# A transformer block in one kernel: PSUM banks of one tag taken in turn by three, the row of maxima moved to ScalarE, sixteen small sums moved to VectorE, two idle products fewer

## Chip, cores and metric

The kernel runs on one core of one Trainium2 chip. The metric is the device time of one launch in microseconds, the median of the runs. Smaller is better.

## What is computed

A block of a diffusion transformer on 16 batches of 256 tokens with 256 features, 16 heads of 16 features each, everything in float32:

```
shift_a, scale_a, gate_a, shift_m, scale_m, gate_m = split(silu(c) @ W_mod + b_mod, 6)
q, k, v = split(modulate(ln(x), shift_a, scale_a) @ W_qkv + b_qkv, 3)
x = x + gate_a * (softmax(q k^T / 4) v @ W_proj + b_proj)            # self-attention, 256 x 256 per head
q = ln(x) @ W_qc + b_qc;  k, v = split(ln(context) @ W_kvc + b_kvc, 2)
x = x + softmax(q k^T / 4) v @ W_cproj + b_cproj                     # cross-attention, 256 context rows
x = x + gate_m * (gelu(modulate(ln(x), shift_m, scale_m) @ W_mlp1 + b_mlp1) @ W_mlp2 + b_mlp2)
```

`ln(t) = (t - mean) * rsqrt(var + 1e-6)`, and `modulate(t, shift, s) = t * (1 + s) + shift`.

## The kernel before

**Units and beats.** The attention work is cut into 32 units: a self-attention unit (kind `s`) and a cross-attention unit (kind `c`) for each batch, in the order s0 to s4, then s5, c0, s6, c1 and so on, and c11 to c15 at the end. The main loop runs over the units `n`, and in each over eight beats `k` (`beat(n, k)`, line 1076). Almost every instruction is pinned to the program order of its engine, so the order written in `beat` is the order in which each engine works.

In beat `k` of unit `n`, `visit` (line 1054) puts on TensorE:
- the scores of unit n+1 for the maxima, four products into the tile `sp` (shown as `s` in the profile), which VectorE reduces to `mx`;
- the transposed scores of unit n for a pair of heads, four products into `st`, of which ScalarE takes the exponential into `pt` (`exp`, called through `exps()`).

Beside these, a beat holds work for other units. In beats 0, 2, 4 and 6, `av_part` multiplies the exponentials with v (tile `o`, 16 products on 32 columns each), and some beats have transposes of normalised inputs (`psT_...`). The projections run as "lanes" (line 444): each product is done in halves of 64 rows, and two projections share the array, one in the upper half of the rows and one in the lower half. `lanes(x, y)` starts x and finishes y, and `run` issues its twelve steps. The order is Q of unit n+2 from beat 1 on, the output projection P of unit n-2 from beat 3, K of unit n+3 from beat 5, and V of unit n+3 from beat 6 or 7.

**The row of maxima.** The softmax subtracts a maximum that is put as a row of its own into q: `m_turn` transposes `mx` on TensorE, `m_row` negates it, and a DMA from SP's queue writes it into q. For the second half of a unit this is in beat 0, for the first half of the next unit in beat 4. When the unit three ahead is a cross-attention unit (`lx` is set), beat 4 writes the transpose into `sp[:, 0]`, ahead of the four transposes of `lx.T[1].turn()`, and `m_row` works on VectorE between the two halves of `q2.Q.low`. Otherwise it has a tile of its own (`psm_...`), and `m_row` works on ScalarE.

**PSUM.** `st` and `sp` take two banks each. The other four banks are shared by two tags, `gen` (`LONG`) and `tr` (`SHORT`), with two buffers each. The projections and the first MLP product take `LONG`; the transposes, `o` and `psm` take `SHORT`. A tile waits until the buffer that it is given has been read.

**Low parts.** Projections are done in three products of rounded high and low parts. `Q.high` rounds on ScalarE (`h_q`, `h_qc`), and `Q.low` subtracts on VectorE (`l_q`, `l_qc`); with these two a projection's bank has been read. The same holds for K.

**Layer norms.** `layernorm` (line 312) takes statistics on VectorE (`st_`, `mv_`), adds epsilon and takes the power -1/2 on GpSimd (`rs_`, in `pow`), and applies both on GpSimd (`xn_`). The names `c0` to `c15` and `q0` to `q15` are those of the context and of the cross-attention's queries.

**Beginning and end.** The beginning is a list of words in `PRE`, issued in order; the word `b12` is twelve products of zeros on TensorE (`busy`, tile `wz`), of two weight loads each, ahead of the transpose of the bias rows (`brow`) and that of the activated condition (`turn`). After the units, the MLP runs over chunks of hidden features, with `mlp_first` (tile `ph`), two gelu passes on ScalarE, a subtraction on GpSimd, and `mlp_second` into `sp` and `st` in turn.

All operations are recorded through one helper, so that the profile gives them line 51; they are told apart by the names of their tiles.

Of the kernel before, what the change touches and what calls it, by code (L numbers as in the profile page):

```python
# [21 lines left out]
def pixart_block(  # L22
# [29 lines left out]
                return tc.keep_in_program_order(i) if self.on else i  # L52
            return issue

    E_ = {'M': ((-46, -37, -26, -24, -20), (-26, -17, -10, -8, 1), (-3, 1, 4, 7, 9), (8, 11, 13, 15)), 'LN': {'s': 'pool', 'c': 'pool', 'q': 'pool'}, 'ON': (1, 1, 1), 'H': (7, 11, 14, 15), 'AP': 23, 'DV': (1, 2), 'E': (-14, -6, -2, 2), 'HP': (1, 0, 2), 'W1P': [(-9, 3), (-8, 3), (-7, 3), (-6, 3), (-4, 5), (-4, 7), (-3, 1), (-3, 5)], 'W2P': [(-4, 3), (-4, 7), (-3, 2), (-3, 4), (-3, 6), (-3, 7), (-2, 2), (-2, 4), (-2, 6), (-1, 0)], 'PRE': 'z0qp z0kp load ld2 ld3 rest one0 silu b12 brow L0a turn L0b b1 L0d scale hik lok T0t z1kp b2 shift T0h T0l ldm hiq loq hiv b1 bk K0a K0m L1a L1b lov L2a L2b z1qa bq K0h K0x K0ya L1e K0l K0s Q0a Q0m Q0h Q0x0 Q0y0a T1t Q0l Q0s0 Q0r T1h V0a V0b T1l bv L2c L3a L3b L3p L3c K1a K1b', 'SL': {(-1, 0): 'Q1a Q1b K1x K1y K1l K1s', (-1, 1): 'T2t T2h T2p V1a Q1x Q1y Q1l Q1s', (-1, 2): 'V1b cpm2', (-1, 3): 'rest z2ka', (-1, 4): 'M0 rest one1 ld4', (-1, 5): 'K2a vone', (-1, 6): 'K2m z2qa', (-1, 7): 'rest c1 one2', (0, 0): 'cpm0 b3 rest', (0, 1): 'rest', (0, 4): 'rest', (1, 0): 'rest', (1, 2): 'rest', (1, 4): 'rest'}}
# [7 lines left out]
    psum = ctx.enter_context(tc.tile_pool(name="psum", bufs=2, space=bass.MemoryType.PSUM))  # L63

    LONG, SHORT = "gen", "tr"
    ps_turn = [0]

    def ps_gen(name, tag=None):


        if tag is None and ps_turn[0] is not None:
            ps_turn[0] ^= 1
            tag = (SHORT, LONG)[ps_turn[0]]
        tag = tag or SHORT
        return psum.tile([P, 512], F32, tag=tag, name=name, bufs=2)


    wz = const.tile([P, P], F32, name="wz")
# [230 lines left out]
    class Box:  # L309
        pass  # L310

    def layernorm(src, name):

        o = Box()
# [12 lines left out]
                o.pow()  # L327

        def pow():
            POOL.tensor_scalar(o.rs, o.mv[:, :, 1], EPS, None, ALU.add)  # L330
            POOL.tensor_tensor(o.rs, o.rs, mhalf, ALU.pow)

        def apply(eng=E_['LN'].get(name[0])):
# [141 lines left out]
    def to_stack(W, src, bias, dst, which, name):  # L475
# [24 lines left out]
        def low(between=None):  # L500
            if name == "k0":
                gap(work, 64, "gap_l")
            o.lo = work.tile([P, KC, N], F32R, tag="qkl", name=f"l_{name}", bufs=3)
            if name == "k0":
                gap(work, 192, "gap_mx")
            for f in range(KC):
                if f and between:
                    between()
# [32 lines left out]
    def to_v(W, src, vt, name):  # L541
        o = Box()
        o.W, o.src, o.tok, o.name = W, src, True, f"v_{name}"

        def first():
            o.ps = ps_gen(f"psv_{name}", SHORT)
            mm3_tok(o.ps[:, 0:H], src.xT, 0, W)

        def second():
            mm3_tok(o.ps[:, H:], src.xT, 1, W)  # L550
            keep()

# [174 lines left out]
        PE.transpose(pst[:16, :P], u.mx[:, hf].rearrange("p r a t -> p (r a t)"), ident)  # L727
        return pst

    def m_row(u, hf, pst, dve=False):  # L730

        m = work.tile([16, P], F32R, tag="m", name=f"m_{u.n}_{hf}", bufs=1)
        if dve:
            DVE.tensor_scalar(m, pst[:16, :P], -1.0, None, ALU.mult)
        else:
            ACT.mul(m, pst[:16, :P], -1.0)
        SP.dma_start(u.q[63:P:64, 4 * hf:4 * hf + 4, :].bitcast(F32), m.bitcast(F32))

    def t_part(u, pair, par):
# [23 lines left out]
    def in_turn(*pieces):  # L763

        for _ in range(2):
            for f in pieces:
                next(f)
# [308 lines left out]
    def beat(n, k):  # L1076
# [20 lines left out]
        if k == 6:  # L1097
            if q2 and not n:
                q2.V.keep()
            if p2 and not alone:  # L1100
                p2.end()
        visit(n, k)
        if k == 0:
            exps()
            if prev:
# [66 lines left out]
        elif k == 4:  # L1172
# [16 lines left out]
            if q3 and q3.kind == "c":  # L1189
                q3.T[0].rest_pool()  # L1190
# [4 lines left out]
                ls.ready = True  # L1195
        elif k == 5:
            exps()
            run(lanes(q3 and q3.K, (None if alone else p2) if n else q2.V))
            if cur:
                o_out(cur, 0)  # L1200
            if lc:
# [38 lines left out]
                p2.add()  # L1240
                p2.store()

    ps_turn[0] = None
    for n in range(-1, nu):
        ACT.on = E_['ON'][0] or n >= nu - 1
        for k in range(8):
# [98 lines left out]
```

## Time and profile before

| | |
|---|---|
| median of 3 runs | 726.04 us (725.52 to 727.03) |
| the profiled execution | 726.2 us |
| its span, first to last instruction | 724.4 us |
| granted TensorE clock, mean | 0.998 |
| TensorE products busy | 712.4 us, 98% of the span |
| TensorE weight loads busy | 592.1 us, 82% |
| VectorE busy | 563.6 us, 78% |
| ScalarE busy | 553.1 us, 76% |
| GpSimd busy | 542.8 us, 75% |

A row of the timeline gives the start in us from the span's start, the duration, the engine (PE is TensorE, PEld its weight loads, DVE VectorE, ACT ScalarE, POOL GpSimd, SP the queue of SyncE), the line, the operation, the tiles as out<-in, the shapes, the count, and in brackets the idle time before it with what ended it. A product's weight load starts just before the product, so PEld rows show when TensorE takes up a piece of work. "issue" is idle time for which the profile shows no wait.

### The profile page before, as it was taken

How to read it: one execution, taken by the hardware profiler on the slowest of the kernel's cores; microseconds unless marked ns; L12 is line 12 of the kernel's file. 1: busy time of each engine (PE TensorE's matmuls, PEld its weight loads, DVE VectorE, ACT ScalarE, POOL GpSimd, SP SyncE). 2: the span in 40 equal slices, each digit the busy share in tenths (PEclk: the TensorE clock that was granted, in tenths of full speed). 3: DMA queues.
4: the chain of work that ended last, by engine and by line, in shares of the span. 5: the costliest groups of instructions: out<-in, count | busy, mean ns of one | idle time of the engine just before them, and what ended most of it. 6: DMA issues, size and time to landing. Idle time of an engine off the chain costs nothing.

```text
span 724.4 us, 22550 instructions
## 1 busy us (share of the span) xinstructions
PE 712.4 (98%) x9007; PEld 592.1 (82%) x9007; DVE 563.6 (78%) x892; ACT 553.1 (76%) x955; POOL 542.8 (75%) x533
## 2 busy tenths in 40 slices
PE   9999999999999999999999999999999999999996
PEld 8777777777777777777777777777679999999996
DVE  5878888888888888888888888888665777777743
ACT  5577888888888888888888888888767677666661
POOL 8465688887867867787786898998766989666561
PEclk9999999999999999999999999999999999999999
DMA  8465455554545555453555656455332223322122
GB/s 261 154 211 175 151 167 176 173 163 165 186 137 179 171 188 171 165 186 135 193 166 184 200 167 201 150 192 190 92 92 87 84 62 85 69 66 88 55 49 73
DMA packets 81531, 106.14 MB, mean 147 GB/s; under 512 B 16594, under 2 KB 44532, under 8 KB 81428
## 3 DMA queue, kind: packets, MB, share of 16 engines
q1 hardware_dynamic: 80420, 104.12, 44.4%
q8 instruction: 71, 1.16, 0.7%
q10 hardware_dynamic: 1008, 0.59, 0.3%
q14 instruction: 32, 0.26, 0.1%
HBM read 35.89 MB, written 8.98 MB: 62 GB/s over the span
## 4 chain that ended last, share of the span: by engine, by line
PE 93%; DVE 4%; ACT 1%; DMA 1%; issue 1%; SPq 0%; ACTq 0%
PE s L51 19%; PE o L51 15%; PE st L51 14%; PE ph L51 12%; PE ps_k L51 4%; PE ps_qc L51 3%; PE ps_q L51 3%; PE ps_v_c L51 3%; PE ps_kc L51 3%; PE ps_P_s L51 3%; DVE mx L51 3%; PE ps_v_s L51 3%; PE ps_P_c L51 2%; PE psT_c L51 2%; PE psT_s L51 2%; PE psT_m L51 1%
## 5 line engine op out<-in xcount | busy, mean ns | idle before, releaser
L51 DVE TENSOR_REDUCE mx<-s 128x4 f32<-128x1024 f32 x252 | 307.9, 1222 | 83.0 <-PE s L51 78.8
L51 ACT ACTIVATE pt<-st 128x1024 f32<-128x1024 f32 x256 | 264.2, 1032 | 58.1 <-PE st L51 56.8
L51 PE MATMUL o<-pt,v 128*32 128x256 f32 x2048 | 137.0, 385 | 0.0
L51 PE MATMUL s<-big 63*128 63x256 f32 x1008 | 117.2, 306 | 2.2 <-DVE mx L51 0.8
L51 PE MATMUL st<-big 64*128 64x256 f32 (+1 forms) x1040 | 107.0, 280 | 0.7 <-ACT pt L51 0.7
L51 PE MATMUL ph<-xTh_m,wself 128*128 128x256 f32 x512 | 99.5, 280 | 0.0
L51 POOL TENSOR_TENSOR hl<-hf,hh 128x512 fp32r<-128x512 f32 x60 | 81.0, 1368 | 19.7 <-ACT hh L51 19.7
L51 PEld LDWEIGHTS s<-big 63*128 63x128 f32 x1008 | 77.4, 185 | 21.8 <-issue 8.5
L51 PEld LDWEIGHTS o<-pt,v 128*32 128x32 f32 x2048 | 53.4, 109 | 39.2
L51 PEld LDWEIGHTS st<-big 64*128 64x128 f32 (+1 forms) x1040 | 81.5, 186 | 3.6 <-ACT pt L51 2.1
L51 PEld LDWEIGHTS ph<-xTh_m,wself 128*128 128x128 f32 x512 | 82.0, 188 | 1.2 <-issue 0.4
L51 PE MATMUL ph<-xTl_m,wself 128*128 128x256 f32 x256 | 70.9, 277 | 0.0
L51 ACT ACTIVATE hh<-ph,bT 128x256 fp32r<-128x256 f32 x112 | 47.4, 479 | 19.0 <-PE st L51 7.4
L51 ACT ACTIVATE hf<-ph,bT 128x256 f32<-128x256 f32 x112 | 47.2, 475 | 19.3 <-PE ph L51 19.2
L51 PEld LDWEIGHTS ph<-xTl_m,wself 128*128 128x128 f32 x256 | 48.2, 188 | 0.0
L51 PE MATMUL s<-big,hh 128*128 128x256 f32 x256 | 45.2, 277 | 0.0
L51 DVE TENSOR_SCALAR xn_m<-x,mv_m,rs_m 128x256 f32<-128x256 f32 x28 | 33.5, 1236 | 14.8 <-POOL rs_m L51 14.8
L51 POOL TENSOR_SCALAR xn_c<-c,mv_c,rs_c 128x256 f32<-128x256 f32 x32 | 39.0, 1229 | 1.7
L51 PE MATMUL st<-big,hh 128*128 128x256 f32 x224 | 39.5, 276 | 0.0
L51 POOL TENSOR_SCALAR xn_q<-x,mv_q,rs_q 128x256 f32<-128x256 f32 x31 | 37.8, 1229 | 1.7
L51 ACT COPY oT<-o 128x512 f32<-128x512 f32 x64 | 37.6, 587 | 1.4 <-PE o L51 1.4
L51 PEld LDWEIGHTS s<-big,hh 128*128 128x128 f32 x256 | 38.6, 188 | 0.0
(229 smaller groups left out, 2121.1 us busy)
## 6 DMA issues: line engine op xcount, KB each, us to landing
big<-h_kc SPq DMA_DIRECT2D x32, 256.0 KB
big<-h_qc SPq DMA_DIRECT2D x32, 256.0 KB
big<-h_k SPq DMA_DIRECT2D x31, 256.0 KB
big<-h_q SPq DMA_DIRECT2D x30, 256.0 KB
big<-l_k SPq DMA_DIRECT2D x16, 256.0 KB
g<-gd SPq DMA_DIRECT2D x16, 256.0 KB
U_s<-oT SPq DMA_DIRECT2D x32, 128.0 KB
c<-in_ctx_dram SPq DMA_DIRECT2D x16, 256.0 KB
```

Of the source, the lines that this page charges most:

```text
L51: i = f(*a, **k)
```

## The change

- The tag `SHORT` has three buffers, and `LONG` one. Q, K and the first MLP product take `SHORT`; the projections to token rows (V and P) and most of the MLP's transposes take `LONG`. Transposes, `o` and `psm` stay with `SHORT`.
- In beat 4 with `lx`, the transpose of the maxima goes into `st[:, 0]`, behind the four transposes, and `m_row` works on ScalarE. In beat 5 with `lx`, two of the twelve lane steps are issued between the products of `s` and those of `st`.
- For the norms `c8` to `c15` and `q8` to `q15` epsilon is added on VectorE, as (var + eps) max var; the power stays on GpSimd.
- `b12` in the beginning is `b10`.

```diff
-    E_ = {... 'PRE': 'z0qp z0kp load ld2 ld3 rest one0 silu b12 brow L0a turn ...
+    E_ = {... 'PRE': 'z0qp z0kp load ld2 ld3 rest one0 silu b10 brow L0a turn ...
...
-    ps_turn = [0]
-    def ps_gen(name, tag=None):
-        if tag is None and ps_turn[0] is not None:
-            ps_turn[0] ^= 1
-            tag = (SHORT, LONG)[ps_turn[0]]
-        tag = tag or SHORT
-        return psum.tile([P, 512], F32, tag=tag, name=name, bufs=2)
+    def ps_gen(name, tag=SHORT):
+        return psum.tile([P, 512], F32, tag=tag, name=name, bufs=1 if tag == LONG else 3)
...
+    eased = [f"{c}{b}" for c in "cq" for b in range(8, B)]
...
         def pow():
-            POOL.tensor_scalar(o.rs, o.mv[:, :, 1], EPS, None, ALU.add)
+            if name in eased:
+                DVE.scalar_tensor_tensor(o.rs, o.mv[:, :, 1], EPS, o.mv[:, :, 1], ALU.add, ALU.max)
+            else:
+                POOL.tensor_scalar(o.rs, o.mv[:, :, 1], EPS, None, ALU.add)
             POOL.tensor_tensor(o.rs, o.rs, mhalf, ALU.pow)
...
-            x.ps, x.fresh = ps_gen(f"ps_{x.name}", LONG), True
+            x.ps, x.fresh = ps_gen(f"ps_{x.name}", LONG if x.tok else SHORT), True
...
-            o.ps = ps_gen(f"ps_{name}", LONG)         # to_stack: Q, K
+            o.ps = ps_gen(f"ps_{name}", SHORT)
...
-            o.ps = ps_gen(f"psv_{name}", SHORT)       # to_v
+            o.ps = ps_gen(f"psv_{name}", LONG)
...
-        pst = ps_gen(f"psT_m{b}", LONG if b < 2 else SHORT)
+        pst = ps_gen(f"psT_m{b}", SHORT if b == 2 else LONG)
...
-        ph = ps_gen(f"ph_{b}_{c}", LONG).rearrange("p (j n) -> p j n", j=2)
+        ph = ps_gen(f"ph_{b}_{c}", SHORT).rearrange("p (j n) -> p j n", j=2)
...
-    def visit(n, k, home=sp):
+    def visit(n, k, home=sp, between=None):
...
         in_turn(*s)
+        if between:
+            between()
         in_turn(*t)
...
-        visit(n, k)
+        kp = None
+        if k == 5 and lx and n:
+            kp = lanes(q3.K, None if alone else p2)
+        visit(n, k, between=kp and (lambda: run(kp, 2)))
...
-            if nxt:
-                pst = m_turn(nxt, 0, sp[:, 0] if lx else None)
             if lx:
                 lx.T[1].turn()
-            if nxt and not lx:
-                m_row(nxt, 0, pst)
+            if nxt:
+                m_part(nxt, 0, st[:, 0] if lx else None)
             if q2:
-                q2.Q.low((lambda: m_row(nxt, 0, pst, True)) if lx else None)
+                q2.Q.low()
...
-            run(lanes(q3 and q3.K, (None if alone else p2) if n else q2.V))
+            run(kp or lanes(q3 and q3.K, (None if alone else p2) if n else q2.V))
```

More of the change, by code (lines that the diff above doesn't have):

```diff
@@ L53, in __getattr__ @@
             return issue
-    E_ = {'M': ((-46, -37, -26, -24, -20), (-26, -17, -10, -8, 1), (-3, 1, 4, 7, 9), (8, 11, 13, 15)), 'LN': {'s': 'pool', 'c': 'pool', 'q': 'pool'}, 'ON': (1, 1, 1), 'H': (7, 11, 14, 15), 'AP': 23, 'DV': (1, 2), 'E': (-14, -6, -2, 2), 'HP': (1, 0, 2), 'W1P': [(-9, 3), (-8, 3), (-7, 3), (-6, 3), (-4, 5), (-4, 7), (-3, 1), (-3, 5)], 'W2P': [(-4, 3), (-4, 7), (-3, 2), (-3, 4), (-3, 6), (-3, 7), (-2, 2), (-2, 4), (-2, 6), (-1, 0)], 'PRE': 'z0qp z0kp load ld2 ld3 rest one0 silu b12 brow L0a turn L0b b1 L0d scale hik lok T0t z1kp b2 shift T0h T0l ldm hiq loq hiv b1 bk K0a K0m L1a L1b lov L2a L2b z1qa bq K0h K0x K0ya L1e K0l K0s Q0a Q0m Q0h Q0x0 Q0y0a T1t Q0l Q0s0 Q0r T1h V0a V0b T1l bv L2c L3a L3b L3p L3c K1a K1b', 'SL': {(-1, 0): 'Q1a Q1b K1x K1y K1l K1s', (-1, 1): 'T2t T2h T2p V1a Q1x Q1y Q1l Q1s', (-1, 2): 'V1b cpm2', (-1, 3): 'rest z2ka', (-1, 4): 'M0 rest one1 ld4', (-1, 5): 'K2a vone', (-1, 6): 'K2m z2qa', (-1, 7): 'rest c1 one2', (0, 0): 'cpm0 b3 rest', (0, 1): 'rest', (0, 4): 'rest', (1, 0): 'rest', (1, 2): 'rest', (1, 4): 'rest'}}
+    E_ = {'M': ((-46, -37, -26, -24, -20), (-26, -17, -10, -8, 1), (-3, 1, 4, 7, 9), (8, 11, 13, 15)), 'LN': {'s': 'pool', 'c': 'pool', 'q': 'pool'}, 'ON': (1, 1, 1), 'H': (7, 11, 14, 15), 'AP': 23, 'DV': (1, 2), 'E': (-14, -6, -2, 2), 'HP': (1, 0, 2), 'W1P': [(-9, 3), (-8, 3), (-7, 3), (-6, 3), (-4, 5), (-4, 7), (-3, 1), (-3, 5)], 'W2P': [(-4, 3), (-4, 7), (-3, 2), (-3, 4), (-3, 6), (-3, 7), (-2, 2), (-2, 4), (-2, 6), (-1, 0)], 'PRE': 'z0qp z0kp load ld2 ld3 rest one0 silu b10 brow L0a turn L0b b1 L0d scale hik lok T0t z1kp b2 shift T0h T0l ldm hiq loq hiv b1 bk K0a K0m L1a L1b lov L2a L2b z1qa bq K0h K0x K0ya L1e K0l K0s Q0a Q0m Q0h Q0x0 Q0y0a T1t Q0l Q0s0 Q0r T1h V0a V0b T1l bv L2c L3a L3b L3p L3c K1a K1b', 'SL': {(-1, 0): 'Q1a Q1b K1x K1y K1l K1s', (-1, 1): 'T2t T2h T2p V1a Q1x Q1y Q1l Q1s', (-1, 2): 'V1b cpm2', (-1, 3): 'rest z2ka', (-1, 4): 'M0 rest one1 ld4', (-1, 5): 'K2a vone', (-1, 6): 'K2m z2qa', (-1, 7): 'rest c1 one2', (0, 0): 'cpm0 b3 rest', (0, 1): 'rest', (0, 4): 'rest', (1, 0): 'rest', (1, 2): 'rest', (1, 4): 'rest'}}
     PE = InOrder(nc.tensor, True)
@@ L498, in high, with low @@
                 ACT.activation(o.hi[:, f], o.ps[:, f * N:(f + 1) * N], AF.Identity, bias=bias[f])
-        def low(between=None):
+        def low():
             if name == "k0":
@@ L506, in low @@
             for f in range(KC):
-                if f and between:
-                    between()
                 DVE.scalar_tensor_tensor(o.lo[:, f], o.ps[:, f * N:(f + 1) * N], bias[f], o.hi[:, f],
@@ L728, in m_turn, with m_row @@
         return pst
-    def m_row(u, hf, pst, dve=False):
+    def m_row(u, hf, pst):
         m = work.tile([16, P], F32R, tag="m", name=f"m_{u.n}_{hf}", bufs=1)
[L733 to L736, printed above, removed]
+        ACT.mul(m, pst[:16, :P], -1.0)
         SP.dma_start(u.q[63:P:64, 4 * hf:4 * hf + 4, :].bitcast(F32), m.bitcast(F32))
@@ L1241, in beat @@
                 p2.store()
-    ps_turn[0] = None
     for n in range(-1, nu):
```

## The prediction

> **What bounds the kernel now.** I read the page first, then the list of waits and the answers by tile, then the timeline of single beats, one engine at a time.
>
> ```profile
> span 724.4 us, 22550 instructions
> PE 93%; DVE 4%; ACT 1%; DMA 1%; issue 1%; SPq 0%; ACTq 0%
> ```
>
> TensorE carries 93% of the chain that ended last. What a change is worth is therefore how long TensorE stands still at the places it touches. The profiled execution took 726.2, which is 1.8 more than its span and 0.2 above the median of 726.04; I add the differences to the median.
>
> In every beat TensorE has s (scores for the maxima), st (scores for the exponentials), projections, and in even beats the products with v. VectorE must reduce s and ScalarE must take the exponential of st before the next beat may write there, so three engines run in step. Two kinds of beat 4 to 5 matter. In one, the unit three ahead is a self-attention unit ("s-unit" below); in the other it is a cross-attention unit ("c-unit").
>
> **The s-unit.**
>
> ```profile
> 328.44 0.09 PEld L51 LDWEIGHTS psm<-ident,mx 128*16 128x16 f32 x1 [0.41 <-issue]
> 328.65 0.30 PEld L51 LDWEIGHTS s<-big 63*128 63x128 f32 x4
> 328.89 0.30 PEld L51 LDWEIGHTS st<-big 64*128 64x128 f32 x4
> 329.40 0.18 PEld L51 LDWEIGHTS ps_k<-xTh_s,wself 64*128 64x128 f32 x1 [0.21 <-DVE l_qc L51]
> ...
> 330.76 0.32 PEld L51 LDWEIGHTS s<-big 63*128 63x128 f32 x4
> ```
> ```profile
> 328.81 0.27 ACT L51 ACTIVATE m<-psm 16x128 fp32r<-16x128 f32 x1
> ```
> ```profile
> 328.49 0.87 DVE L51 SCALAR_TENSOR_TENSOR l_qc<-ps_qc,bP,h_qc 128x256 fp32r<-128x256 f32 x2
> 329.27 1.21 DVE L51 TENSOR_REDUCE mx<-s 128x4 f32<-128x1024 f32 x1
> ```
> ```profile
>   DVE l_qc L51: 2.3, 10
>   DVE l_q L51: 0.5, 2
> ```
>
> K of the unit three ahead goes into the bank that Q of the unit two ahead leaves. The low half of that Q is finished at 328.49 + 0.87 = 329.36, and K starts at 329.40. After s, st started 0.24 later (328.65 to 328.89); by the same step K could have started at 329.13, so it is late by 0.27. With three turning banks another one is free: that of psm, which ScalarE has read by 328.81 + 0.27 = 329.08. If K gets it, the 0.27 goes. What is late next is the reduction: it ends at 329.27 + 1.21 = 330.48, so the next s can start at 330.53 instead of 330.76, and the gain is 0.23. The last two rows count 10 + 2 such waits: 12 x 0.23 = **2.8 us won**. The ends are 0, if K still gets Q's bank, and 12 x 0.27 = 3.2. I take 2.8, since psm's bank comes free 0.28 before Q's.
>
> V and P, which now turn in a single bank, stand in beats 6 to 2 and 3 to 6; each starts after the other has been read, so I cost that at nothing. The cover is those beats' distance; were it gone, it would be one read of a bank, about 0.6, in each unit.
>
> **The c-unit.** Here the row of negated maxima m leaves the s bank and VectorE, and goes to the st bank and ScalarE; two steps of the projections are pulled between s and st of beat 5.
>
> ```profile
> 311.50 0.59 PEld L51 LDWEIGHTS o<-pt,v 128*32 128x32 f32 x16
> 312.66 0.09 PEld L51 LDWEIGHTS s<-ident,mx 128*16 128x16 f32 x1 [0.57 <-DVE mx L51]
> 312.73 0.42 PEld L51 LDWEIGHTS psT_q<-ident,xn_q 128*128 128x128 f32 x4
> 313.32 0.30 PEld L51 LDWEIGHTS s<-big 63*128 63x128 f32 x4 [0.17 <-DVE m L51]
> 313.55 0.31 PEld L51 LDWEIGHTS st<-big 64*128 64x128 f32 x4
> ...
> 319.05 0.31 PEld L51 LDWEIGHTS st<-big 64*128 64x128 f32 x4
> ```
> ```profile
> 311.94 1.05 ACT L51 ACTIVATE pt<-st 128x1024 f32<-128x1024 f32 x1
> 314.17 1.03 ACT L51 ACTIVATE pt<-st 128x1024 f32<-128x1024 f32 x1 [1.18 <-PE st L51]
> 315.10 0.58 ACT L51 COPY oT<-o 128x512 f32<-128x512 f32 x1
> 315.56 0.60 ACT L51 COPY t_s<-ps_P_s 128x512 f32<-128x512 f32 x1
> 316.04 1.06 ACT L51 ACTIVATE pt<-st 128x1024 f32<-128x1024 f32 x1
> 316.95 0.62 ACT L51 CAST xTh_q<-psT_q 128x512 fp32r<-128x512 f32 x1
> 317.42 0.64 ACT L51 COPY y_q<-psT_q 128x512 f32<-128x512 f32 x1
> 317.90 1.10 ACT L51 ACTIVATE pt<-st 128x1024 f32<-128x1024 f32 x1
> ```
> ```profile
> L51 DVE TENSOR_SCALAR m<-s 16x128 fp32r<-16x128 f32 x16 | 4.5, 278 | 0.0
> ```
>
> The wait removed is small: 0.57 of idle loading before m, against 0.41 at psm in the s-unit, where nothing is waited for. So TensorE is ready at 312.66 - 0.16 = 312.50. In the new order the four transposes go first and take 0.42, until 312.92. Then m must wait for the exponential that reads st, until 311.94 + 1.05 = 312.99, and starts at about 313.04. By psm's spacing, s follows 0.21 later at 313.25 and takes 0.23. The two steps take 0.11 each (in the s-unit twelve such steps lie between 329.40 and 330.76). So st starts at 313.71, where it was 313.55. TensorE has done two steps more by then and has lost nothing. ScalarE's reading of m, 0.27, fits into the 1.18 that it idles. I estimate its end near 313.64, with 0.3 for the product itself (from m at 312.66 to the s behind it at 313.32, less the 0.28 that VectorE's reading takes in the last row). But the exponential of beat 5 now starts at 314.17 + 0.16 = 314.33, and from there to the exponential of beat 7 the ScalarE rows leave no idle time: each starts as the last ends. That last one ends at 317.90 + 1.10 = 319.00, and st of the next beat starts 0.05 later, at 319.05, without slack to speak of. So the 0.16 comes out there; I take off 0.04 for what slack there is. That is 0.12 in each of 16 c-units, **2.0 us lost** with the last of them, whose exponential is later still. The ends: a gain of 0.1 each (1.6 won) if st of beat 5 comes no later than now, and 0.26 each (4.2 lost) if ScalarE takes up m 0.10 later than that and this adds to the 0.16. Nearest are the rows that I added up.
>
> SP's queue gets the DMA of m before that of the low half of Q, as now; m is 0.3 later, and is read from beat 0 on, some 5 us on, so nothing waits.
>
> **The epsilon sums.** Sixteen additions on two numbers for each partition, for cross-attention from batch 8 on, leave GpSimd for VectorE, which reads the variance twice from memory.
>
> ```profile
> 12.72 1.31 POOL L51 TENSOR_TENSOR wself<-wf,wself 128x512 fp32r<-128x512 f32 x1
> ```
> ```profile
> 13.01 1.03 DVE L51 SCALAR_TENSOR_TENSOR nb_s<-mv_s,rs_s 128x2 f32<-128x2 f32 x1
> ```
> ```profile
> 485.74 0.16 DVE L51 SCALAR_TENSOR_TENSOR nb_q<-mv_q,rs_q 128x2 f32<-128x2 f32 x1 [0.52 <-POOL rs_q L51]
> ```
> ```profile
> 433.87 0.23 DVE L51 BATCH_NORM_AGGREGATE mv_q<-st_q 128x2 f32<-128x6 f32 x2
> 434.02 1.20 DVE L51 TENSOR_REDUCE mx<-s 128x4 f32<-128x1024 f32 x1
> ```
> ```profile
> 434.02 1.28 POOL L51 TENSOR_TENSOR xTl_as<-U_s,xTh_as 128x512 fp32r<-128x512 f32 x1
> ```
> ```profile
> 435.46 0.30 PEld L51 LDWEIGHTS s<-big 63*128 63x128 f32 x4 [0.17 <-issue]
> ```
>
> The same instruction on the same shape took 0.16 once and 1.03 once. The long one began inside a GpSimd instruction (12.72 to 14.03) and ended with it, at 14.04. I read it as held until GpSimd was done. On the timeline of GpSimd most of the sixteen places find it idle or about to end; the worst is at 434.10, where the statistics end and GpSimd has just begun 1.28. Held, the sum runs from 435.30 to 435.46, and the reduction behind it in VectorE's queue, now from 434.02 to 435.22, ends near 436.6. TensorE's s at 435.46 waits for it: 1.1 lost. For the other fifteen I estimate 0.06 each, 0.9, between nothing (VectorE idles before its next reduction) and 1.1. Together **2.0 us lost**; the ends are 0 and 4. GpSimd's saved additions lie beside TensorE's work.
>
> The Trainium skill, "SBUF — State Buffer", section "Who interferes with whom", says that a VectorE instruction with two SBUF inputs and a GpSimd instruction that reads SBUF exclude each other for a whole instruction, and that whichever starts first wins. This trace's 1.03 beside 0.16 agrees; the rule speaks against this part of the change.
>
> **The idle products.**
>
> ```profile
> 1.84 2.98 PEld L51 LDWEIGHTS s<-wz 128*128 128x128 f32 x14
> 1.03 4.45 PEld L51 LDWEIGHTS s<-wz 128*128 128x128 f32 x24 [1.03 <-DVE wz L51]
> 5.61 0.13 PEld L51 LDWEIGHTS s<-ident,brow 32*128 32x128 f32 x1
> 6.53 0.73 DVE L51 TENSOR_SCALAR xn_s<-x,mv_s,rs_s 128x256 f32<-128x256 f32 x2 [1.15 <-POOL rs_s L51]
> ```
>
> Twelve products are 24 loads. Fourteen of them take 2.98, some 0.21 each; all 24 in 4.45 means that the last go at about 0.11. Four fewer let the bias transpose start 0.45 before 5.61. The first activations still come at 6.53 + 0.73 = 7.26, so their transposes keep their place: nothing won, nothing lost. Ends: 0.45 won, and the clock's case below.
>
> **In the MLP** the products turn in three banks instead of two. The waits listed after 546 name no wait of TensorE for a bank, so that is worth nothing.
>
> **Sum.** -2.8 + 2.0 + 2.0 = +1.2, so 726.04 + 1.2 = 727.2. The forecast's own range, with about one unknown each way, is 725.7 to 729.0. I call 0.2% (1.45 us) what a measurement of this kernel can tell from no change.
>
> **Rivals.**
> - *K stays with Q's bank* in the s-units. Which free bank a tile gets is settled when the program is built, and the trace does not show it. For it: Q's bank is as old. Against: psm's is free 0.28 sooner. The 2.8 are not won: 726.04 + 4.0 = 730.0, slower. It decides where K's first load still starts right behind l_q.
> - *One of the two losses is not there*: VectorE is not held (the 1.03 had another cause, or GpSimd has drifted), or st of beat 5 finds the slack. For it: only one long instance exists. -2.8 + 2.0 = -0.8: 725.2.
> - *Both are not there*: 726.04 - 2.8 = 723.2, faster.
> - *The clock steps up later*: with 20 loads instead of 24 the step that the loads show could be missed. Some 25 loads then go at 0.21 instead of 0.11, 2.5, of which other work hides 1: +1.5 on an unchanged kernel, 727.5; on the forecast 728.7. Against: the step came with 17 or so loads. The Trainium skill, "TensorE: Matmul & The Clock Gate", Part 1, has the clock doubling after about 3.4 us of activity; by that rule 20 loads suffice, since they still last longer.
>
> **How the numbers follow.** Forecast 0.42, K's bank 0.14, one loss gone 0.25, both gone 0.12, clock 0.03, something else 0.04. Faster by over 0.2%: both gone 0.12, and a third of "one gone", 0.08, and 0.02 of the rest: 0.22. Slower: K's bank 0.14, the clock 0.03, half of the forecast's spread 0.21, and 0.03: 0.41. The rest, 0.37, is within 0.2%. The range reaches from "both gone" to "K's bank" with their own bounds: 722.8 to 731.0.
>
> **What would show it.** Right: no wait of ps_k for l_q or l_qc; in c-units m behind the four transposes and "pt" named before it, and st of beat 0 later against beat 4 by about 0.1; a VectorE rs_q row of over 1 us near 434, with the s after it waiting for mx. Wrong: rs rows of 0.2 throughout, ScalarE idle between beats 5 and 7, or ps_k still behind l_qc.

## The result and the profile after: slower by 0.7%, and the loss is at the beginning

| | before | changed |
|---|---|---|
| median of 9 runs | 726.78 us | 733.3 us |
| lowest to highest | 725.52 to 729.23 | 727.92 to 737.61 |
| profiled execution | 726.2 (span 724.4) | 729.56 (span 727.8) |
| mean granted clock of that execution | 0.998 | 0.991 |

The ratio of the runs is 1.0068, 95% interval 1.0039 to 1.0097; the two medians by themselves give 1.0090. The forecast was 727.2, the range 722.8 to 731.0: the median lies outside it. Two later measurements of the same kernel gave medians of 730.24 and 730.89, where the kernel before had 727.71 and 726.62: these lie inside the range, at its upper end. So the loss was 6.5, 2.5 and 4.3 us in the three measurements; why the first was the highest no run shows. In this measurement the changed kernel's runs spread over 10 us, those of the kernel before over less than 4.

First the page of the changed kernel: span, TensorE's line and the shares of the chain that ended last.

```profile
span 727.8 us, 22486 instructions
...
PE 717.7 (99%) x9003; PEld 598.2 (82%) x9003; DVE 564.0 (78%) x892; ACT 556.7 (76%) x971; POOL 538.1 (74%) x517
...
PE 89%; DMA 4%; DVE 3%; ACT 2%; POOL 1%; issue 1%; ACTq 0%; SPq 0%; POOLq 0%
```

TensorE still sets the time, but its clock does not stay up. The windows view has, after the busy time of each engine, the granted clock (PEclk), the share of the DMA engines and GB/s:

```profile
4.07:7.48 3.41, 2.97 (x24) 2.46 (x24) 2.13 (x8) 0.97 (x3) 2.06 (x4) 1.00 0.94 277
7.48:21.13 13.65, 13.65 (x65) 13.65 (x65) 4.51 (x18) 6.50 (x12) 9.48 (x10) 0.50 0.68 223
21.13:24.54 3.41, 3.41 (x32) 3.28 (x30) 2.25 (x8) 1.43 (x3) 0.23 (x1) 1.00 0.28 99
```

The clock stepped up at 4.07, was taken back at 7.48 and stayed at one half for 13.65 us. The timeline of the weight loads shows what preceded that, in the same columns as in the prediction:

```profile
1.04 3.73 PEld L51 LDWEIGHTS s<-wz 128*128 128x128 f32 x20 [1.04 <-DVE wz L51]
4.90 0.14 PEld L51 LDWEIGHTS s<-ident,brow 32*128 32x128 f32 x1
4.96 0.20 PEld L51 LDWEIGHTS st<-ident,c_sb 16*128 16x128 f32 x2
5.42 0.30 PEld L51 LDWEIGHTS s<-wz 128*128 128x128 f32 x2 [0.26 <-ACT bT L51]
5.64 0.97 PEld L51 LDWEIGHTS st<-sT,wf 128*128 128x128 f32 x8
6.98 0.14 PEld L51 LDWEIGHTS psT_s<-ident,xn_s 128*128 128x128 f32 x1 [0.37 <-DVE xn_s L51]
7.31 0.38 PEld L51 LDWEIGHTS psT_s<-ident,xn_s 128*128 128x128 f32 x3 [0.18 <-DVE xn_s L51]
7.68 0.97 PEld L51 LDWEIGHTS s<-wz 128*128 128x128 f32 x4
8.53 1.83 PEld L51 LDWEIGHTS st<-sT,wf 128*128 128x128 f32 x8
```

Four loads fewer stand at the beginning, the bias transposes come at 4.90 instead of 5.61 (0.71 sooner, where the prediction had 0.45), and all that was gained is handed back as a wait of 0.37 and another of 0.18 for the first layer norm, xn_s, which VectorE ends when it did before. Then the clock falls: eight loads st<-sT take 0.97 at 5.64 and 1.83 at 8.53. The first scores of unit 0 start at 38.05 instead of 32.98, some 5.1 late. After that the changed kernel wins time: from unit 1 to unit 30 it is 1.17 shorter than before (worked out from the starts of each unit's first st row), and its span ends 3.4 late.

**The s-unit.** The prediction showed ps_k waiting for l_qc at 329.40. The same place two units earlier, in the changed kernel (the kernel before had a wait of 0.24 for l_qc there):

```profile
299.74 0.09 PEld L51 LDWEIGHTS psm<-ident,mx 128*16 128x16 f32 x1 [0.41 <-issue]
299.95 0.30 PEld L51 LDWEIGHTS s<-big 63*128 63x128 f32 x4
300.19 0.31 PEld L51 LDWEIGHTS st<-big 64*128 64x128 f32 x4
300.43 0.18 PEld L51 LDWEIGHTS ps_k<-xTh_s,wself 64*128 64x128 f32 x1
```

K follows st after 0.24 with no wait, and no ps_k waits for a low half any more.

**The c-unit.** TensorE's rows at the moved row of maxima, then ScalarE's over the rest of the unit:

```profile
315.11 0.42 PEld L51 LDWEIGHTS psT_q<-ident,xn_q 128*128 128x128 f32 x4 [0.41 <-issue]
315.64 0.09 PEld L51 LDWEIGHTS st<-ident,mx 128*16 128x16 f32 x1
315.85 0.30 PEld L51 LDWEIGHTS s<-big 63*128 63x128 f32 x4
...
316.32 0.31 PEld L51 LDWEIGHTS st<-big 64*128 64x128 f32 x4
```
```profile
314.55 1.04 ACT L51 ACTIVATE pt<-st 128x1024 f32<-128x1024 f32 x1
315.96 0.27 ACT L51 ACTIVATE m<-st 16x128 fp32r<-16x128 f32 x1 [0.37 <-PE st L51]
316.87 1.03 ACT L51 ACTIVATE pt<-st 128x1024 f32<-128x1024 f32 x1 [0.65 <-PE st L51]
317.80 0.58 ACT L51 COPY oT<-o 128x512 f32<-128x512 f32 x1
318.26 0.60 ACT L51 COPY t_s<-ps_P_s 128x512 f32<-128x512 f32 x1
318.73 1.06 ACT L51 ACTIVATE pt<-st 128x1024 f32<-128x1024 f32 x1
...
320.59 1.10 ACT L51 ACTIVATE pt<-st 128x1024 f32<-128x1024 f32 x1
```

m stands behind the four transposes and starts 0.05 after the exponential has ended at 314.55 + 1.04 = 315.59; its row names no wait. From 316.87 on ScalarE has no idle time to the end of the unit, as the prediction said.

**The epsilon sums.** In this profile 14 of 16 take 0.16 to 0.23; two take 0.83, beside a GpSimd addition:

```profile
428.11 0.83 DVE L51 SCALAR_TENSOR_TENSOR rs_c<-mv_c 128x2 f32<-128x2 f32 x1
428.87 1.21 DVE L51 TENSOR_REDUCE mx<-s 128x4 f32<-128x1024 f32 x1
```
```profile
427.64 1.29 POOL L51 TENSOR_TENSOR x<-xg,t_s 128x512 f32<-128x512 f32 x1
```
```profile
430.13 0.30 PEld L51 LDWEIGHTS s<-big 63*128 63x128 f32 x4 [0.21 <-DVE mx L51]
```

The sum ends 0.01 after the addition does, and s behind it loses 0.21.

### The profile page after: what moved, and what is told of

It is laid out like the page before. It is cut to its first block, busy times and chain, and to the rows that moved or that the text cites. A ratio compares the mean times of both kernels' runs of the same rounds, so it can differ in the third digit from the quotient of the medians.

```text
span 727.8 us, 22486 instructions
## 1 busy us (share of the span) xinstructions
PE 717.7 (99%) x9003; PEld 598.2 (82%) x9003; DVE 564.0 (78%) x892; ACT 556.7 (76%) x971; POOL 538.1 (74%) x517
## 4 chain that ended last, share of the span: by engine, by line
PE 89%; DMA 4%; DVE 3%; ACT 2%; POOL 1%; issue 1%; ACTq 0%; SPq 0%; POOLq 0%
PE s L51 17%; PE o L51 15%; PE st L51 14%; PE ph L51 12%; PE ps_q L51 4%; PE ps_k L51 3%; PE ps_qc L51 3%; PE ps_kc L51 3%; PE ps_v_s L51 3%; PE ps_v_c L51 3%; DVE mx L51 2%; PE ps_P_s L51 2%; PE psT_c L51 2%; DMA R_c<-rd_c 2%; PE ps_P_c L51 2%; PE psT_s L51 2%
## 5 line engine op out<-in xcount | busy, mean ns | idle before, releaser
L51 PE MATMUL st<-big 64*128 64x256 f32 (+1 forms) x1040 | 109.3, 284 | 0.7 <-ACT pt L51 0.7
L51 DVE TENSOR_TENSOR xmg<-x,gm 128x512 f32<-128x512 f32 x16 | 24.0, 1502 | 18.8 <-DMA gm<-gd 18.8
```

Source lines behind the costliest of these rows:

```text
L51: i = f(*a, **k)
```

## The experiments

Medians in us; the kernel before was measured beside each group of four (the last: of two). The groups e1 to e4, e5 to e8 and so on ran at different times and on three chips, and the kernel before had medians of 726.62 to 728.53 in them, so a run is best compared within its group. "Lapsed" is a run whose mean granted clock, recorded from the first step on, is 0.995 or less.

| run | median | runs | kernel before | ratio, 95% interval | lapsed |
|---|---|---|---|---|---|
| e1 changed, 12 products | 727.82 | 12 | 726.98 | 1.0011, 0.999 to 1.0033 | 2 |
| e2 before, 10 products | 729.57 | 12 | 726.98 | 1.0022, 1.0002 to 1.0043 | 2 |
| e3 changed, 12, sums on GpSimd | 726.22 | 12 | 726.98 | 0.9986, 0.9963 to 1.0008 | 3 |
| e4 changed, 16 | 727.79 | 12 | 726.98 | 1.0005, 0.9986 to 1.0024 | 0 |
| e5 changed again | 730.24 | 12 | 727.71 | 1.0022, 0.9997 to 1.0048 | 1 |
| e6 changed, two products more at the norm | 729.34 | 12 | 727.71 | 1.0023, 0.9994 to 1.0052 | 1 |
| e7 before, sums on VectorE | 730.03 | 12 | 727.71 | 1.0025, 1.0001 to 1.005 | 1 |
| e8 banks only | 724.89 | 12 | 727.71 | 0.9946, 0.9922 to 0.9969 | 0 |
| e9 before, 12 + 2 | 728.25 | 12 | 727.93 | 1.0004, 0.998 to 1.0027 | 2 |
| e10 banks, 12 + 2 | 724.27 | 11 | 727.93 | 0.9959, 0.9932 to 0.9987 | 2 |
| e11 banks and row, 12 + 2 | 725.62 | 12 | 727.93 | 0.9964, 0.9944 to 0.9984 | 0 |
| e12 changed, 12 + 2 | 727.6 | 12 | 727.93 | 0.9995, 0.997 to 1.0021 | 1 |
| e13 before, 8 | 733.22 | 6 | 726.62 | 1.0075, 1.0052 to 1.0098 | 3 |
| e14 before, 4 | 732.02 | 4 | 726.62 | 1.0075, 1.005 to 1.0099 | 0 |
| e15 before, 10, again | 729.04 | 8 | 726.62 | 1.0047, 1.0018 to 1.0077 | 1 |
| e16 changed, third time | 730.89 | 8 | 726.62 | 1.0055, 1.0023 to 1.0086 | 4 |
| e17 before, 10, no hold | 734.41 | 5 | 728.53 | 1.0084, 1.0071 to 1.0097 | 0 |
| e18 banks, 12 + 2, no hold | 732.91 | 6 | 728.53 | 1.0064, 1.0051 to 1.0077 | 0 |

### The products and the parts (e1 to e4)

```diff
e1, from the changed kernel
-    'PRE': '... silu b10 brow ...'
+    'PRE': '... silu b12 brow ...'
e2, from the kernel before
-    'PRE': '... silu b12 brow ...'
+    'PRE': '... silu b10 brow ...'
e3, from e1
-    eased = [f"{c}{b}" for c in "cq" for b in range(8, B)]
+    eased = [f"{c}{b}" for c in "" for b in range(8, B)]
e4, from the changed kernel
-    'PRE': '... silu b10 brow ...'
+    'PRE': '... silu b16 brow ...'
```

> The changed kernel with the two idle products put back (twelve ahead of the first transpose). Theory A, the clock: in the changed kernel's trace the granted clock falls to one half at 7.48 us and stays there for 13.65 us, after a window of 3.41 us in which TensorE stood idle three times (0.13, 0.26 and 0.37 us); the first scores came 5.08 us late, while the rest of the kernel (from the first unit to the MLP stage) was 1.8 us shorter than before. With twelve products there is no half clock after the step-up, the first scores come within 0.2 us of the kernel before (32.98 us), and the time is 724.4 us where the kernel before has 726.2, ratio 0.9975. Theory B, the products are innocent and the late start comes from the new banks: the first scores come 5 us late here too, and the time stays at 730 to 733 us, ratio 1.005 or above.

> The kernel before with two of the twelve idle products left out and nothing else changed. Theory A, the clock: a half clock after the step-up in the profile or a step-up that comes one window later, first scores 3 to 7 us later than 32.98 us, runs spread over several us, median 730 to 735 us, ratio 1.006 to 1.010. Theory B, the products are innocent: 726 to 727 us, ratio 1.000, first scores at 33.0 us.

> The changed kernel with twelve idle products and all epsilon sums on GpSimd, as before the change. The changed kernel's trace has two epsilon sums of 0.83 us on VectorE instead of 0.16 us, and its units 24 and 26 lose 0.36 and 0.40 us more than the other self-attention units. Theory A, that is all the sums cost: this kernel is 0.7 to 0.9 us faster than the one with the sums on VectorE, 723.6 us, ratio to the kernel before 0.9965. Theory of the prediction, 2.0 us: 722.4 us. Theory C, a late mean and variance held up GpSimd before the change and the late sums on VectorE repair that: the sums pay, and this kernel is 0.5 us or more slower than the one with the sums on VectorE.

> The changed kernel with sixteen idle products, four more than before the change. Theory A, the clock, a matter of how much of the window is busy: no half clock in any run, the first transpose 8 loads of 0.11 us later (0.9 us at most), part of it hidden by the wait for the first layer norm, so 0 to 0.9 us above the kernel with twelve products and a spread no larger than that of the kernel before. Theory D, the place of the products counts and not their number: the half clock comes in some runs here too, and the median is 3 us or more above the one with twelve.

The two products carry most of the loss: put back, the changed kernel is 0.8 above the kernel before instead of 6.5 (2.5 and 4.3 in the later measurements); taken from the kernel before, they cost 2.6 there, in two groups: six runs at 728.5 or less, six at 730.6 to 732.1. Its profile caught one of the first group. Theory B falls: in e1's profile the first scores come at 33.85, 0.87 late, though not within theory A's 0.2. And e1 missed its 724.4, since the sums cost more in this profile than in the first: five of sixteen take 0.36 to 1.01. One of them stands where the prediction had put the worst, near 434 (VectorE, GpSimd, TensorE of e1):

```profile
433.27 0.89 DVE L51 SCALAR_TENSOR_TENSOR rs_q<-mv_q 128x2 f32<-128x2 f32 x1
434.09 1.21 DVE L51 TENSOR_REDUCE mx<-s 128x4 f32<-128x1024 f32 x1
```
```profile
432.86 1.29 POOL L51 TENSOR_TENSOR xTl_as<-U_s,xTh_as 128x512 fp32r<-128x512 f32 x1
```
```profile
435.35 0.30 PEld L51 LDWEIGHTS s<-big 63*128 63x128 f32 x4 [0.98 <-DVE mx L51]
```

The sum lasts until 434.16, 0.01 after GpSimd's instruction, and s loses 0.98. Back on GpSimd (e3), the sums save 1.6 by the medians, twice theory A's 0.7 to 0.9, near the prediction's 2.0, though the two intervals overlap; theory C finds no support. e4 has no lapse in 12 runs, as theory A said, though one run took 730.36.

### The change again, the place of the products, and two parts alone (e5 to e8)

```diff
e5 is the changed kernel; e6, from the changed kernel
-    'PRE': '... scale hik lok T0t ...'
+    'PRE': '... scale b2 hik lok T0t ...'
e7, from the kernel before
+    eased = [f"{c}{b}" for c in "cq" for b in range(8, B)]
...
+            if name in eased:
+                DVE.scalar_tensor_tensor(o.rs, o.mv[:, :, 1], EPS, o.mv[:, :, 1], ALU.add, ALU.max)
+            else:
+                POOL.tensor_scalar(o.rs, o.mv[:, :, 1], EPS, None, ALU.add)
-            POOL.tensor_scalar(o.rs, o.mv[:, :, 1], EPS, None, ALU.add)
e8, from the kernel before (and the tags at the callers as in the change)
-        return psum.tile([P, 512], F32, tag=tag, name=name, bufs=2)
+        return psum.tile([P, 512], F32, tag=tag, name=name, bufs=1 if tag == LONG else 3)
```

> The changed kernel as it is, beside the next three on the same chip. Up to here the kernel before with ten products (729.6 us) is 2.6 us above the kernel before, and the changed kernel with twelve is 727.8 us. Theory A (ten products leave the half clock to chance, in this kernel as in that one): the median lies 2 to 5 us above 727.8 us, some runs at 725 to 728 and some at 730 to 737 us, and the profile either has a half clock of 13.65 us near the beginning or first scores within 1.5 us of 33.0 us. Theory F (the ten products cost 2.6 us and something else in the changed kernel the rest): the runs lie close together and the units after the first are longer than in the first profile of this kernel, where they were 1.8 us shorter than before.

> The changed kernel with two more idle products right ahead of the first layer norm's transposes, where TensorE stood idle for 0.37 us; still ten at the very beginning, as many in all as before the change. Theory A in the form that the window's busy share decides: the idle time of the window falls from 0.76 to about 0.4 us, as before the change, the half clock goes, and the median is that of the changed kernel with twelve, 726.5 to 728.5 us. Theory G, the length of the unbroken stretch at the beginning decides: nothing is mended, 729.5 us or more, and a half clock or a late step-up in a good half of the runs.

> The kernel before with the sixteen late epsilon sums on VectorE and nothing else changed (twelve products, old banks). With the other parts of the change, their cost in single profiles was 0.8, 2.4 and 2.5 us, in units 23 to 28, where the sum started while GpSimd was adding and lasted 0.8 to 1.0 us. Theory A, the sums are held up by GpSimd: two to five of the sixteen sums take over 0.5 us, units 23 to 28 are 1 to 2.5 us longer in all, 728.0 to 729.5 us, ratio 1.0015 to 1.0035. Rival: in this kernel's own timing GpSimd is never found busy: all sums 0.16 to 0.23 us, ratio 1.000.

> The kernel before with the three turning banks and the single bank for V and P, and nothing else: same instructions in the same order on every engine, twelve products, epsilon sums on GpSimd, the maxima's row where it was. Theory A, K no longer waits for Q's bank: the self-attention units are 0.25 to 0.30 us shorter each (in beat 5), the others unchanged, 12 to 14 times, 3.3 us in all: 723.7 us, ratio 0.9950 to 0.9965. Rival H, part of the 0.30 us came from moving the row of maxima: 0.1 us or less per unit, ratio above 0.998.

e5 agrees with theory A in its two groups (four runs at 727.2 to 728.1, eight at 730.0 to 733.7), but its profile caught one of the first. e6 decides little: 729.34 lies between the two theories' bounds, with one lapse and four more runs at 730.6 to 735.5, so the products next to the norm do not mend it. e7 confirms the sums' price by itself: 2.3 by the medians, though the interval of the ratio begins at 1.0001; six of the sixteen sums of its profile take 0.37 to 1.05, and units 23 to 27 lose 3.1. e8 confirms the banks: 2.8 won, and its profile is 3.24 shorter from unit 1 to unit 30; rival H falls. Against the kernel before it has the lowest ratio of the study, 0.5% below; only e10 has a lower median.

### Each step on filled TensorE (e9 to e12)

```diff
e9 from the kernel before, e10 from e8, e11 from e3, e12 from e1, each
-    'PRE': '... scale hik lok T0t ...'
+    'PRE': '... scale b2 hik lok T0t ...'
```

> The kernel before with two idle products more, placed right ahead of the first layer norm's transposes (fourteen in all, none left out). Theory A in the form that the count of columns streamed in a window decides: I add up the moving columns of the products that start in each window of 3.41 us, reckoned back and forth from the clock's first step. The window after which the clock fell has 1600; the windows after the step in the other profiles have 1600 to 2240, and this kernel gets 512 more there, at least 1800 wherever the step falls. Then no run falls: the tail of the kernel before (9 of 70 runs above 731 us) is gone, all runs lie within 725.5 to 728.7 us, and the median is within 0.7 us of the kernel before. Rival J, the tail is not the clock: runs above 731 us stay.

> The banks alone (twelve products, sums on GpSimd, row of maxima as before) with the two products more ahead of the first transposes. Theory A: the cost of the banks in quiet clock, 3.2 us less than the filled kernel before by the first profile of the banks (724.9 us by its median), that is 723.0 to 724.0 us, and a spread of under 3.5 us. Rival H2, the banks' gain was the luck of that job's clock: no more than 1.5 us below the filled kernel before.

> Banks and the moved row of maxima (with its two early projection steps), all sums on GpSimd, twelve products and two more ahead of the first transposes. Less the banks alone this is the price of the moved row. The prediction's step: 2.0 us more than the banks alone. By the single profiles: 0.05 us net in each of 15 cross-attention units (0.15 lost in beat 4, 0.21 won in beat 5, 0.13 lost by the chain of exponentials) and 0.64 in the last, 1.4 us. Theory K, the 1.23 us that one profile lost in unit 25 to a late layer norm of GpSimd belongs to the moved row too: 2.5 us or more.

> The whole change but for the products: banks, moved row and sums on VectorE, with twelve products and two more ahead of the first transposes. Theory A: with the clock quiet the changed kernel is what the prediction's other three steps make of it, 0 to 1.5 us above the filled kernel before (the prediction's sum is +1.2), no run above 730 us, and 1.0 to 2.5 us above the one with the sums on GpSimd. Rival F, something beside the clock makes the changed kernel slow: 2.5 us or more above the filled kernel before, or runs up to 733 us.

As a ladder of medians the three steps are 728.25, 724.27 (banks), 725.62 (row of maxima), 727.6 (sums): -4.0, +1.4, +2.0. All but the products, the change is within a microsecond of the kernel before (e12, and e12 against e9), and rival F falls by the median. Its tail is still there: one run of e12 lapsed to 733.14 and two took 730.1 and 730.5, where theory A had none above 730. The column form of theory A falls too: e9 and e10 still lapse, twice each. No lapsed run of these was caught in a profile. In e10 the price of a lapse can be seen clean: nine runs within 723.52 to 725.14 with a clock of 0.998 or more, two at 729.89 and 729.95 with 0.991 and 0.995. It is some 5.7. Theory K holds in part: unit 25, where TensorE waits for a layer norm on GpSimd, is 1.07 longer than before in e3's profile and 1.09 in e11's, the two with the moved row and all sums on GpSimd, and not longer by over 0.1 in those of e8 and e10, which have the banks alone. Yet the medians give the row 1.4 in all.

### Fewer products still (e13 to e16)

```diff
e15 is e2 and e16 the changed kernel; e13 and e14, from the kernel before
-    'PRE': '... silu b12 brow ...'
+    'PRE': '... silu b8 brow ...'
...
+    'PRE': '... silu b4 brow ...'
```

> The kernel before with eight idle products (sixteen loads, to about 4.5 us at half clock). Theory A, columns streamed per window: the early windows hold 1,570 columns or fewer after the step wherever it falls, against 1600 in the window after which the clock fell. A lapse or a step later than 7.3 us in most runs; first scores 3 to 7 us later than 33.0 us; median 730 to 733 us. Theory L (what makes the ten products slow has another cause than the clock's first 20 us): no more than the kernel with ten, 729.6 us, and first scores at 33 to 34 us in its profile.

> The kernel before with four idle products (eight loads, 1.7 us at half clock). Theory A: the first step cannot come at the window's end that the kernel before uses, since no window up to 7 us holds 1,600 columns; it comes at 7.5 to 14 us or later. First scores 4 to 9 us late, median 731 to 736 us, the mean clock from the first step on 0.998 or more in part of the runs although they are slow. Theory L: within 2 us of the kernel with ten products, and a step before 7.3 us.

> The kernel before with ten products once more, for a profile of another run. If its time is above 730 us with a mean clock of 0.998 or more: by theory A its first step comes later than 7.3 us and its first scores 3.5 us or more later than 33.0 us, with the units after that as before; by theory L the first scores come at 33 to 34 us and the units are longer. If its time is under 729 us it says nothing new.

> The changed kernel once more, for a profile of another run. As for the one before: above 731 us with a mean clock of 0.998 or more, theory A puts the first step later than 7.3 us and the first scores 3.5 us or more later than 33.0 us; theory L has them at 33 to 34 us.

Both doses act nearly as theory A expected (e13's median and its first scores lie a little beyond the bounds), and theory L falls. In e14's profile the clock's first step comes at 16.71, and the first scores 4.06 late, with a mean clock of 0.998: a late step does not show in that mean. The loads show it, half as fast from the first to the last of these:

```profile
1.04 1.78 PEld L51 LDWEIGHTS s<-wz 128*128 128x128 f32 x8 [1.04 <-DVE wz L51]
4.87 0.17 PEld L51 LDWEIGHTS s<-ident,brow 32*128 32x128 f32 x1 [2.05 <-POOL big L51]
...
9.14 1.83 PEld L51 LDWEIGHTS st<-sT,wf 128*128 128x128 f32 x8
...
11.36 1.78 PEld L51 LDWEIGHTS st<-cpT,wf 128*128 128x128 f32 x8
```

e13's profile showed something that no theory had. Its step came at 23.91, the first scores 7.96 late, and this stands before it (TensorE, VectorE, GpSimd):

```profile
7.46 0.37 PEld L51 LDWEIGHTS psT_s<-ident,xn_s 128*128 128x128 f32 x1
10.16 0.50 PEld L51 LDWEIGHTS psT_s<-ident,xn_s 128*128 128x128 f32 x3 [2.33 <-DVE xn_s L51]
```
```profile
6.54 3.57 DVE L51 TENSOR_SCALAR xn_s<-x,mv_s,rs_s 128x256 f32<-128x256 f32 x2 [1.15 <-POOL rs_s L51]
```
```profile
6.92 1.29 POOL L51 TENSOR_TENSOR wself<-wf,wself 128x512 fp32r<-128x512 f32 x1 [0.42 <-ACT wself L51]
8.15 1.81 POOL L51 MEMSET big<- 128x2048 f32 x1
```

The two halves of the layer norm took 0.73 in the kernel before and 3.57 here: the second was held until GpSimd was through with two instructions, the first of which began 0.06 into it. In the kernel before that one begins at 7.19, behind ScalarE's cast of the weights, and the norm is nearly done. What decides looks like who comes first: in e13 GpSimd began at 6.92, before the first half had ended at 6.95. In the profiles of e6, e14 and e16 it began at 6.96 to 7.00, the second half took its 0.41, and GpSimd's instruction took 1.42 to 1.47 instead of 1.30. That fewer products bring this on is not shown: the cast starts at 6.20 in e13 and at 6.45 in the kernel before, but in both it waited for the DMA of the weights and not for ScalarE's bias work. The hold was caught in this one profile. e15 and e16 caught no late run in their profiles; three of e15's runs took over 730 with a clock of 0.998 or 0.999.

### The hold taken away (e17, e18)

```diff
+    late = const.tile([P, 2], F32, name="late")
+    word["xnd"] = lambda: POOL.tensor_scalar(late, u0.ln[0].xn[:, 1, 0:2], 0.0, None, ALU.add)
e17, from e2
-    'PRE': '... scale hik lok T0t ...'
+    'PRE': '... scale hik xnd lok T0t ...'
e18, from e10
-    'PRE': '... scale b2 hik lok T0t ...'
+    'PRE': '... scale b2 hik xnd lok T0t ...'
```

> The kernel before with ten idle products, and one GpSimd instruction on two numbers for each partition put ahead of the first weights' low half: it reads the second half of the first layer norm, so that GpSimd cannot start on the weights before VectorE is done with it. That delays the low half by 0.1 to 0.6 us. Of 20 runs with ten products and without it, 10 took over 730 us. Theory M, the hold makes the slow runs: at most 2 of 12 over 730 us (as with twelve products), median 726.5 to 728 us. Theory A, the columns: 4 to 8 of 12 over 730 us, median 728.5 to 731 us.

> The version to be recommended: the banks alone, twelve products and two more ahead of the first transposes, and the GpSimd instruction that keeps the hold away. Without that instruction 2 of 11 runs lapsed to 729.9 us and the others lay within 723.5 to 725.1 us. Theory M: no lapse, all runs within 723.5 to 725.6 us, median 724.2 us, 0.9950 of the kernel before. Theory A or another cause: lapses of some 5.5 us remain in 1 to 3 of 12.

Both theories' medians were missed, and the medians say nothing of the question. The beginning went as wanted (first scores of e17 at 33.28), but the products run slower, above all in the MLP: from the end of the attention units on, both kernels lose some 6 us against the profile of the kernel before. The windows of one and the same 80 us of the MLP, e17 and then the kernel before (second and third columns: TensorE busy time and count of its products and loads):

```profile
560.00:640.00 80.00, 80.00 (x681) 80.00 (x680) 58.73 (x88) 55.28 (x131) 63.64 (x56) 1.00 0.27 79
```
```profile
560.00:640.00 80.00, 80.00 (x706) 80.00 (x705) 60.32 (x90) 56.57 (x134) 65.87 (x57) 1.00 0.28 74
```

That is a load every 0.1176 us instead of every 0.1135, at full clock in both. The new tile may have moved later tiles in memory; no run shows whether that is the cause. Of the question only the spread can be read: all five runs of e17 lie within 0.8 us and none lapsed, where ten products without that instruction had gone over 730 in 10 of 20 runs; none of e18's six lapsed. That speaks for theory M, but eleven runs of slower kernels on another chip do not settle it.

## Why the prediction was wrong

**The idle products: the step that failed.** "Nothing won, nothing lost" followed the transposes, which did keep their place, and left out what the time between them does to the clock. The rival with a later step had a chance of 0.03 and a price of 1.5. It was argued away by the length of the products: 20 loads outlast the step. True, the step came at 4.07 in the profile. What was missed is that the clock is judged again after the step, and that the wait in front of psT_s, which follows from the prediction's own rows, lies in the next window. A profile with twelve products and nearly the same step shows the difference: in e3's the clock stepped up at 4.01 and stayed up. Its next window, in the columns of the windows above:

```profile
4.01:7.42 3.41, 3.25 (x27) 2.84 (x27) 2.19 (x8) 1.01 (x4) 1.75 (x3) 1.00 0.94 300
```

TensorE was busy for 3.25 us there instead of 2.97. The step itself came anywhere from 4.01 to 6.55 in the profiles with ten or more products, so which window a wait falls into is chance from run to run. But busy time alone is not what the clock goes by. In e15's profile it stayed up through this window:

```profile
13.00:16.41 3.41, 2.40 (x19) 2.01 (x19) 1.90 (x4) 2.58 (x7) 3.13 (x4) 1.00 0.61 167
```

And in e13's TensorE was busy without a gap from 10.25 to 23.91 at half clock before the step came. Most products in e15's window move 256 columns, and eight of those ahead of the fall move only 16 (256 and 16 in the shapes of their rows on PE); the columns may count, but no run separates that.

The price was too small as well: the lapse in the profile lasts 13.65 us and moved the first scores by 5.1; a late step cost 4.06 with four products and, with the held norm, 7.96 with eight. Of 29 runs of the changed kernel 8 lapsed, and 11 more took over 730; with twelve products or more the changed kernel (e1, e4, e12) lapsed in 3 of 36, and 3 more took over 730. The kernel before went over 730 in 13 of the 136 runs that were measured beside these experiments, all of them lapsed.

The Trainium skill, "TensorE: Matmul & The Clock Gate", Part 1, has the clock fall back after an idle window of about 3.4 us. The measurement differs: TensorE was busy for 2.97 of the 3.41 us ahead of the fall.

**K's bank: right.** Forecast -2.8, measured -2.8 (e8) and -4.0 (e10 against e9), and -3.24 in e8's profile; the undisturbed s-units of the changed kernel's profile were 0.26 to 0.37 shorter each.

**The row of maxima: right in mechanism, near in size.** Forecast +2.0, measured +1.4 (e11 against e10, by medians; their intervals against the kernel before overlap). The chain of exponentials is there, and st of beat 0 comes 8.08 after that of beat 4 (313.66 to 321.74), which was 7.99. The term that was missed pays: the two steps done early make beat 5 shorter by 0.21, so that a c-unit loses some 0.06 on average and not 0.12. The last place loses 0.44 in the changed kernel's profile and 0.34 in e11's, since there the exponential starts late and m waits for it, as the prediction had it everywhere (TensorE, then ScalarE):

```profile
490.76 0.09 PEld L51 LDWEIGHTS st<-ident,mx 128*16 128x16 f32 x1 [0.55 <-ACT pt L51]
```
```profile
489.67 1.04 ACT L51 ACTIVATE pt<-st 128x1024 f32<-128x1024 f32 x1
```

**The epsilon sums: right in size.** Forecast +2.0, measured +1.6 (e1 against e3), +2.0 (e12 against e11), +2.3 (e7); each alone is hardly clear of the noise, but the three agree. Wrong was to price one place at 1.1 and fifteen at 0.06. GpSimd's phase differs from run to run: two to six sums were held for a good part of GpSimd's instruction, and in the changed kernel's first profile the place near 434 was not among them. That the total came out near is in part luck. The Trainium skill's rule that the prediction named, "SBUF — State Buffer", section "Who interferes with whom", is borne out by these rows.

**V, P, the MLP's three banks and SP's queue: nothing, as forecast.** From the last exponential to the end the changed kernel's profile lost 0.1, and beats 0 to 3 of six of its c-units kept their length to within 0.02 on average.

**The sum.** Without the products' term the forecast was +1.2; e1 gives +0.8 and e12 -0.3, both within its own range (-0.3 to +3.0); against e9, which has the same fourteen products, e12 is at -0.65, just below it. Of the first measurement's 733.3, 0.7 is the kernel before's own median, 726.78 where the forecast started from 726.04.

**What stays open.** How much of the products' price is the window alone (the changed kernel's first profile: no hold, and yet a lapse) and how much begins with the held layer norm (e13). What the clock counts in a window. Only one lapse was caught in a profile, and no late step of the changed kernel itself; that its runs above 730 with a full mean clock had one is inferred from e14.

## What to carry to other kernels

Idle products at the beginning are not only there to raise the clock once: here, those that also filled part of the window after the step kept it up more often, and a mean clock that is recorded from the first step on hides a step that comes late. Before you take out work that looks idle, ask what in the next microseconds depends on it. Of this change keep the banks, which won 2.8 us alone, and leave the sums, the row of maxima and the products as they were.

## What the hardware did that was not expected

- The clock fell at 7.48 after a window in which TensorE was busy for 2.97 of 3.41 us, and stayed at one half for 13.65 us although it was busy throughout (the changed kernel's profile). In another profile (e15) it stayed up through a window of 3.41 us with TensorE busy for 2.40.
- Half a layer norm, 0.41 us on VectorE, lasted 3.24 (e13): it ended only after the GpSimd instruction that it collided with and the next one, a memset of 1.81.
- One more tile of two numbers for each partition, with the GpSimd instruction that writes it, went with a load every 0.1176 instead of 0.1135 us in 80 us of the MLP (e17); the cause is not shown.
